# A graph layer on one core: 16-bit column addresses, more columns copied per octet, and the octet's nodes copied on the chip

## The chip, the core and the metric

The kernel runs on one core of a Trainium2 chip. A core has TensorE (PE, matrix products; PEld is its weight load), VectorE (DVE), ScalarE (ACT), GpSimd (POOL) and SyncE (SP, which only issues transfers). Each has its own queue of instructions; they meet through semaphores. Data lie in SBUF (128 partitions), products in PSUM, inputs in HBM. The metric is the device time of the one core in microseconds. Three runs of the kernel before took 3439.3 to 3445.99 us, median 3443.22.

## The reference

One message-passing layer of a graph network, with a residual and a layer norm: 12500 nodes with 64 features, 400000 edges with 16 features, edges sorted by their target `dst`.

```
m_in     = concat([x[src], x[dst], edge_attr], -1)
h        = silu(m_in @ W1 + b1)
messages = silu(h @ W2 + b2)
agg      = segment_sum(messages, dst, 12500)
z        = silu(concat([x, agg], -1) @ W3 + b3)
out      = layernorm(x + z)
```

All is float32. `x[src]` is a gather with random indices; `x[dst]` and the sum are local, since `dst` is sorted.

## The kernel before

**Tiles and octets.** The 400000 edges are 3125 tiles of 128 edges. Eight tiles are an octet (`OT`); there are 391 octets (`NO`). Three octets are a chunk (`CT`), for which target indices and edge features are loaded at once (`load`, tiles `dr` and `oh`). The loop over octets is written out, and inside `tc.manual_schedule` the order on TensorE, ScalarE, VectorE and SyncE is the order of the code. Iteration `o` works on several octets in different stages: the first layer of octet `o`, the second of `o - 2`, the sums over targets of `o - 4`, and preparations for `o + 1` to `o + 3`.

**An octet's stages.** `compare_dst` (L447, VectorE) builds a one-hot matrix that says which of the 48 nodes of the octet's window an edge has as target. `window_load` (L415, SP) brings x of these 48 nodes, transposed and twice, into the tile `xr`; `window_product` (L420, TensorE) multiplies it by the part of W1 for targets; `window_copy` (L425, VectorE) puts the product into one of three weight tiles `xw`. `first_layer` adds up, in PSUM, the transposed gathered rows (L476) and the product of `xw` with the one-hot matrix and the edge features (L480); ScalarE applies silu (L483, `h`). `second_layer` does the same with W2 (L492, L494, silu at L498, `m`). `compare_nodes` (L453, VectorE) builds the one-hot matrix for the sum; `add_up` (L507, TensorE) makes the sums of an octet in `pg`; `add_window` (L512, VectorE) adds them to the resident sums `agg` at a column read from a register.

**Where x[src] comes from.** From octet `RAW` = 12 on, a table `pa = x @ W1[:64]` lies in HBM. Three sources share the edges:

- POOL gathers most tiles with one indirect DMA per tile (`gather`, L396), three octets ahead.
- In the octets of the list `pairs`, the first two tiles are not gathered. Their 256 columns of x are copied out of `xs`, x transposed, which is resident in SBUF, into a tile `cx` (`columns`: ScalarE L303, VectorE L301), one copy of four bytes in 64 partitions per edge. The address of each copy is a register. The registers are filled by loads (L294) from a row of addresses in SBUF, 16 or 8 at a time. TensorE multiplies `cx` by W1 (L479).
- In the octets of `rpairs`, two more tiles come as single rows of `pa`, one SP transfer each (`rows`, L347), 16 per octet.

ScalarE copies `ACOLS` = 32 + 28 columns per octet, before the two silus, and VectorE `VCOLS` = 32 + 32, behind `compare_dst` and behind `compare_nodes`. These are 124 per octet, so a pair of tiles takes 2.06 octets. `index` loads the 256 source indices of a pair as 32-bit integers (SP, L374), `address` (L382, VectorE, two operations of 128) makes addresses of them in place: 4 x index plus the base of `xs`, and, for the second tile, plus a partition offset. For that second tile `xs` holds x a second time in partitions 64 to 127, loaded in octets 5 to 8 (`resident(1, c)`).

**Nodes.** When the sums of 512 nodes are complete, they go through `node_load`, `node_product` (L539 to L542), `node_silu` (L548, tile `z`), `node_stats` (L555 to L559) and, in batches, the norm (`divide`, L572) and `store`. Which octet does which of these is worked out beforehand and kept in the dictionary `todo`; it is run at the end of an iteration.

**Order on VectorE in an iteration:** `add_window`, `compare_dst`, `columns` part 0, `window_copy`, `compare_nodes`, `columns` part 1, `address`, node work. On ScalarE: columns part 0, h, columns part 1, m, node work. On SP: `index`, `rload`, `load` of a chunk two octets ahead, `window_load` three octets ahead, `rows`.

Of the kernel before, what the change touches and what calls it, by code (L numbers as in the profile page):

```python
# [9 lines left out]
F32 = mybir.dt.float32  # L10
BF16 = mybir.dt.bfloat16
I32 = mybir.dt.int32
U8 = mybir.dt.uint8
AF = mybir.ActivationFunctionType
OP = mybir.AluOpType
AX = mybir.AxisListType
# [2 lines left out]
ENG = mybir.EngineType  # L19

P = 128
# [9 lines left out]
LAST = 6  # L31
RAW = 12
TABLES = 7
ACOLS = (32, 28)
VCOLS = (32, 32)
ROWS = 16
LOADS = (16, 8)
XBASE = (0, 64 << 18)
XADDR = 36864
LAG = CT * P // 32  # L40

U = 125
# [58 lines left out]
def windows(ctx, tc, ident, badi, pa, x, xt, src_c, src_row, dst_c, dst_row, attr_t, dst_2, attr_2, base, w1, b1, w2, b2, w3, b3, out, edges):  # L101
# [5 lines left out]
    NO = base.shape[1]  # L107
    assert 2 * (S + A) == P and N + S <= NP
    E = 2 * S
    const = ctx.enter_context(tc.tile_pool(name="fconst", bufs=1))  # L110

    fast = ctx.enter_context(tc.tile_pool(name="fast", bufs=1))
    scp = ctx.enter_context(tc.tile_pool(name="scp", bufs=3))
    srcs = {}

    def sources(k, part=None):
# [24 lines left out]
        nc.scalar.dma_start(w1d[h, h], w1[0:D, :])  # L141
        nc.scalar.dma_start(b1s[h, :], b1.rearrange("(k o) -> k o", o=1))
    XC = 2048
    xs = fast.tile([P, NP], F32, name="xs")

    def resident(s, c):
        w = min(XC, NP - c)
        nc.scalar.dma_start(xs[s * D:(s + 1) * D, c:c + w], xt[:, c:c + w])

    resident(0, 0)  # L150
    for s in range(2):
        h = slice(s * D, (s + 1) * D)
        nc.scalar.dma_start(w2d[h, h], w2)
    resident(0, XC)
    w3x = const.tile([D, D], F32, name="w3x")
    b3r = const.tile([1, G, D], F32, name="b3r")

# [93 lines left out]
    with tc.tile_pool(name="gat", bufs=AHEAD + 2) as gat, tc.tile_pool(name="drp", bufs=2) as drp, \  # L251
# [4 lines left out]
            tc.tile_pool(name="ps1", bufs=2, space=PSUM) as ps1, \  # L256
            tc.tile_pool(name="ps2", bufs=2, space=PSUM) as ps2, \
            tc.tile_pool(name="psa", bufs=1, space=PSUM) as psa, \
            tc.tile_pool(name="cx", bufs=4) as cx, tc.tile_pool(name="cxi", bufs=3) as cxi, \
            tc.tile_pool(name="rx", bufs=2) as rx, tc.tile_pool(name="rxi", bufs=2) as rxi, \  # L260
            tc.tile_pool(name="nx", bufs=2) as nx, tc.tile_pool(name="nv", bufs=1) as nv:
        got, loaded, made = {}, {}, {}
# [2 lines left out]
        RATE = sum(ACOLS) + sum(VCOLS)  # L265
        pairs = []
        while True:
            o = RAW + -(-2 * P * (len(pairs) + 1) // RATE) + 1
            if o >= len(octs) - 1:
                break  # L270
            pairs.append(o)
        cols, indices = {}, {}
        xb = xs.bitcast(U8)

        def columns(o, eng, part):
            if o < RAW:
                return
            lo = (o - RAW) * RATE
            if eng == ENG.Activation:
                lo, n = lo + sum(ACOLS[:part]), ACOLS[part]  # L280
            else:
                lo, n = lo + sum(ACOLS) + sum(VCOLS[:part]), VCOLS[part]
            hi, todo = lo + n, n
            while lo < hi:
# [9 lines left out]
                _, regs = nc.values_load_multi_w_load_instructions(  # L294
                    indices[j][0:1, e0:e0 + n], engines=(eng,), min_val=XBASE[s] + XADDR,
                    max_val=XBASE[s] + XADDR + 4 * (N - 1), skip_runtime_bounds_check_because="src names a node")
                for e, r in zip(range(e0 % P, e0 % P + n), regs):
                    to, frm = t[h, 4 * e:4 * e + 4], xb[h, ds(r - (XBASE[s] + XADDR), 4)]
                    if eng == ENG.DVE:

                        nc.vector.tensor_reduce(to, frm[:, :, None], AX.X, OP.max)  # L301
                    else:
                        nc.scalar.copy(to, frm)  # L303
                lo += n


        def begun(o):

            first, behind = -(-(o - RAW) * RATE // (2 * P)), -(-(o + 1 - RAW) * RATE // (2 * P))
            return range(max(0, first), max(0, min(behind, len(pairs))))  # L310

        def index(o):
            for j in begun(o):
                t = cxi.tile([1, 2 * P], I32, name="cxi")
                e = octs[pairs[j]][1] * P
                nc.sync.dma_start(t, src_row[:, e:e + 2 * P])
                indices[j] = t

        def address(o):
            for j in begun(o):  # L320
                t = indices[j]
                for s in range(2):
                    h = slice(s * P, (s + 1) * P)
                    nc.vector.tensor_scalar(t[:, h], t[:, h], 4.0, float(XBASE[s] + XADDR), op0=OP.mult, op1=OP.add)

        rpairs = []
        while True:
# [48 lines left out]

        def address(o):
            for j in begun(o):
                t = indices[j]
                for s in range(2):  # L380
                    h = slice(s * P, (s + 1) * P)
                    nc.vector.tensor_scalar(t[:, h], t[:, h], 4.0, float(XBASE[s] + XADDR), op0=OP.mult, op1=OP.add)  # L382

        winrow, winreg = {}, {}
        sums = psa.tile([P, 4, S], F32, name="pg")
# [15 lines left out]
        def bases(eng, o):  # L401

            n = min(4, NO - o)
            _, regs = nc.values_load_multi_w_load_instructions(
                bi[0:1, o:o + n], engines=(eng,), min_val=0, max_val=N - 1,
                skip_runtime_bounds_check_because="dst names a node")
            for i in range(n):
                winreg[eng, o + i] = regs[i]

        def window_load(o):  # L410
            if o % 4 == 0:
                bases(ENG.SP, o)
            xr = win.tile([D, 2, S], F32, name="xr")
            frm = xt[:, ds(winreg.pop((ENG.SP, o)), S)]
            nc.sync.dma_start(xr, frm[:, None, :].to_broadcast([D, 2, S]))  # L415
            winrow[o] = xr

        def window_product(o):
# [5 lines left out]
        def window_copy(o):  # L424
            nc.vector.tensor_tensor(xw[o % 3][:E, :], winrow.pop(o)[:E, :], mask[:E, :], op=OP.mult)  # L425
# [159 lines left out]
        todo = {}  # L585

        def later(o, f, *a):
            todo.setdefault(min(o, NO), []).append((f, a))
# [4 lines left out]
        for q in range(early):  # L593
            o = lead[due[q]] + LAST - 1 if q < rest else NO
            later(o - 1, node_load, q)
            later(o, node_product, q)
            later(o, node_silu, q)
            later(o + 2, node_stats, q)
        for q0, q1 in batches:
            o = lead[due[q1 - 1]] + LAST - 1  # L600
# [22 lines left out]
        with tc.manual_schedule(engines={ENG.PE, ENG.Activation, ENG.DVE, ENG.SP}):  # L623
            compare_dst(0)
            compare_nodes(0)
            for o in range(NO + THIRD):
# [5 lines left out]
                    nc.scalar.activation(agg[:, k:k + n], zero.to_broadcast([P, n]), AF.Copy)  # L632
                if o < 2:
                    for c in parts[2:5] if o == 0 else parts[5:]:
                        resident(0, c)
# [7 lines left out]
                if o == RAW:  # L643
                    nc.vector.memset(mv, 1.0)
                    nc.vector.memset(eps, 1e-5)
                if 5 <= o < 5 + (len(parts) + 1) // 2:
                    for c in parts[(o - 5) * 2:(o - 4) * 2]:
                        resident(1, c)
                index(o + 3)
                rload(o + 3)  # L650
                if o % (SCT // OT) == 6 and (o // (SCT // OT) + 1) * SCT < TILES:
                    sources(o // (SCT // OT) + 1)
                if o + AHEAD < NO:
                    gather(o + AHEAD)
                if o + 2 < NO and octs[o + 2][3] and o + 2:
                    load(octs[o + 2][0])
                if o + 3 < NO:
                    window_load(o + 3)
                if o + 1 < NO:
                    window_product(o + 1)  # L660
                if o % 4 == 0 and 4 <= o < NO + 4:
                    bases(ENG.DVE, o - 4)
                if o >= LAST:
                    add_window(o - LAST)
                if o + 1 < NO:
# [1 line left out]
                columns(o, ENG.DVE, 0)  # L667
                if o < NO:
                    first_layer(o)
                if o == 0:  # L670
                    nc.vector.tensor_copy(b2r, b2p[:, None, :].to_broadcast([3, OT, D]))
                if o + 1 < NO:
                    window_copy(o + 1)
                    compare_nodes(o + 1)
                columns(o, ENG.DVE, 1)
                if o == 1:
                    relative(CT, SCT)
                if 10 <= o < 9 + len(cuts):
# [38 lines left out]

        for o in range(NO + THIRD - LAST, NO):
            add_window(o)
        for f, a in todo.get(NO, []):  # L720
            f(*a)
        for q in range(early, NG):
            node_load(q)
            node_product(q)
            node_silu(q)
            node_stats(q)
# [262 lines left out]
```

## Time and profile before

| what | us |
|---|---|
| median of three runs | 3443.22 |
| the profiled execution | 3453.06 |
| its span | 3450.7 |
| ScalarE busy | 2717.7 |
| POOL busy | 2569.0 |
| TensorE matmul busy | 2554.8 |
| VectorE busy | 2517.4 |

The granted TensorE clock was 0.68 of full speed over the span. A row of a group gives the source line, the engine, the operation, output and inputs, the shape and the count; then the busy time in us and the mean duration of one in ns; then how long the engine idled just before, and what ended most of that. "Issue" means that the engine waited for nothing that the profile shows. Short operations overlap in the records, so that the mean of one is longer than the time from start to start. Register loads are not counted as busy.

### The profile page before, as it was taken

To read this page: it belongs to the slowest core of one execution; us is meant where nothing else is said; L and a number is where in the kernel's file an instruction comes from. 1 tells how busy PE (TensorE), PEld (TensorE's weight loads), DVE (VectorE), ACT (ScalarE), POOL (GpSimd) and SP (SyncE) were. 2 spreads that over 40 slices of the span, in tenths; PEclk is the share of its full clock that TensorE was granted. 3 is DMA by queue.
4 is the path that set the end of the run, shared out by engine and by line. 5 is a ranking of instruction groups with operands and counts; after the bars stand their busy time and mean duration, and the time that the engine had idled before them with its cause. 6 is when DMAs were issued, how large, how long until landed. Compare 5 with 4: busy or idle time off the path is not lost. (4 is left out here: it accounts for less than half of the span.)

```text
span 3450.7 us, 104586 instructions
## 1 busy us (share of the span) xinstructions
PE 2554.8 (74%) x13750; PEld 1649.2 (48%) x13750; DVE 2517.4 (73%) x26396; ACT 2717.7 (79%) x23405; POOL 2569.0 (74%) x2724
## 2 busy tenths in 40 slices
PE   6877777777777677776777777777777677677777
PEld 4444544444445445444444445444445454444454
DVE  2477777777777777777777777777777777777775
ACT  2388788788887887888878888887788777878886
POOL 7777777777777777777777777777777777777773
PEclk9666667666667666776666666666666666766767
DMA  7423323323332332333332332333323323333322
GB/s 159 95 53 68 63 59 65 65 61 60 77 61 61 68 62 60 65 65 65 64 69 59 62 68 61 62 75 61 62 60 69 60 61 66 69 62 62 67 61 52
DMA packets 203931, 229.79 MB, mean 67 GB/s; under 512 B 133612, under 2 KB 141988, under 8 KB 202324
## 3 DMA queue, kind: packets, MB, share of 16 engines
q1 hardware_dynamic: 101528, 122.61, 16.1%
q0 software_dynamic: 86880, 89.14, 14.1%
q10 hardware_dynamic: 14812, 11.26, 1.4%
q14 instruction: 595, 4.87, 0.5%
q8 instruction: 116, 1.90, 0.2%
HBM read 216.36 MB, written 6.40 MB: 65 GB/s over the span
## 5 line engine op out<-in xcount | busy, mean ns | idle before, releaser
L396 POOL DMA_INDIRECT ga<-pa,sc x2619 | 2475.4, 945 | 802.2 <-issue 711.9
L303 ACT COPY cx<-xs 64x4 uint8 x22560 | 2216.5, 188 | 166.8 <-issue 122.0
L301 DVE TENSOR_REDUCE cx<-xs 64x4 uint8 x24032 | 1782.6, 150 | 544.7 <-issue 477.8
L507 PEld LDWEIGHTS pg<-eh,m 128*64 128x64 f32 x6250 | 301.0, 182 | 1046.8 <-issue 331.1
L507 PE MATMUL pg<-eh,m 128*64 128x48 f32 x6250 | 351.3, 271 | 580.9 <-DVE agg L512 523.0
L480 PE MATMUL p<-oh,xw 128*128 128x512 f32 (+1 forms) x758 | 601.0, 887 | 132.3 <-DVE xw L425 130.0
L494 PE MATMUL p<-w2d,h 128*128 128x128 f32 x3126 | 674.8, 383 | 0.0
L494 PEld LDWEIGHTS p<-w2d,h 128*128 128x128 f32 x3126 | 573.8, 275 | 133.1 <-issue 133.1
L498 ACT ACTIVATE m<-p 128x512 f32<-128x512 f32 x391 | 232.2, 594 | 255.5 <-PE p L494 249.0
L447 DVE TENSOR_TENSOR oh<-dr,wrow 96x512 f32<-96x512 int32 x391 | 264.4, 676 | 209.1 <-DMA dr<-in_dst 121.6
L483 ACT ACTIVATE h<-p,b1s 128x512 f32<-128x512 f32 x391 | 267.3, 684 | 139.2 <-PE p L480 86.1
L476 PE MATMUL p<-ident,ga 128*128 128x128 f32 x1310 | 336.9, 389 | 41.4 <-DMA ga<-pa,sc 41.4
L420 PE MATMUL mm<-w1bb,xr 64*96 64x128 f32 x782 | 252.9, 418 | 62.0 <-DMA xr<-in_xt 36.7
L476 PEld LDWEIGHTS p<-ident,ga 128*128 128x128 f32 x1310 | 199.6, 190 | 133.3 <-issue 110.3
L480 PEld LDWEIGHTS p<-oh,xw 128*128 128x128 f32 x758 | 176.7, 287 | 169.3 <-DVE xw L425 168.8
L453 DVE TENSOR_TENSOR eh<-wrow,dc 128x384 f32<-128x384 f32 x391 | 211.7, 541 | 0.0
L420 PEld LDWEIGHTS mm<-w1bb,xr 64*96 64x96 f32 x782 | 134.2, 224 | 140.2 <-issue 61.4
L492 PE MATMUL p<-b2r,one 3*128 3x512 bf16 x391 | 196.4, 502 | 0.0
L512 DVE TENSOR_TENSOR agg<-agg,pg 128x48 f32 x391 | 78.1, 200 | 74.2 <-PE pg L507 40.0
L479 PE MATMUL p<-cx,w1d 128*128 128x128 f32 x364 | 105.2, 387 | 22.7 <-ACT cx L303 22.7
L425 DVE TENSOR_TENSOR xw<-mm,mask 96x128 f32<-96x128 f32 x391 | 109.4, 280 | 13.4 <-PE mm L420 7.6
L396 POOL DMA_INDIRECT ga<-in_x,sc x96 | 91.5, 953 | 30.2 <-issue 27.7
(83 smaller groups left out, 767.6 us busy)
## 6 DMA issues: line engine op xcount, KB each, us to landing
rx<-pa SPq DMA_DIRECT2D x5888, 0.2 KB
dr<-in_dst SPq DMA_DIRECT2D x260, 288.0 KB
ga<-pa,sc POOLq DMA_INDIRECT x2619
oh<-in_attr SPq DMA_DIRECT2D x130, 192.0 KB
xr<-in_xt SPq DMA_DIRECT2D x391, 24.0 KB
xs<-in_xt ACTq DMA_DIRECT2D x12, 512.0 KB
pa<-v ACTq DMA_DIRECT2D x12, 256.0 KB
xa<-in_x SPq DMA_DIRECT2D x24, 128.0 KB
```

Of the source, the lines that this page charges most:

```text
L301: nc.vector.tensor_reduce(to, frm[:, :, None], AX.X, OP.max)
L303: nc.scalar.copy(to, frm)
L396: nc.gpsimd.indirect_dma_start(out=ga[:, i, :], out_offset=None, in_=x if o < RAW else pa[:, :], in_offset=bass.IndirectOffsetOnAxis(ap=sc ...
L420: nc.tensor.matmul(pw[:E, :], winrow[o].rearrange("k s w -> k (s w)"), w1bb.rearrange("k s m -> k (s m)"), start=True, stop=True)
L447: nc.vector.tensor_tensor(oh[:E, :], dr[:, e:e + w], wn[:E, o:o + 1].to_broadcast([E, w]), op=OP.is_equal)
L453: nc.vector.tensor_tensor(eh[:, :n], row[:, None, :].to_broadcast([P, n, S]), rel[:, t0:t0 + n, None].to_broadcast([P, n, S]), op=OP.is_equal)
L476: nc.tensor.matmul(p1[:, i, :], g2.rearrange("p s d -> p (s d)"), ident, is_transpose=True, start=(i == c), stop=False, skip_group_check=True)
L480: nc.tensor.matmul(p1[:, :k], xw[o % 3], oh, start=False, stop=True, skip_group_check=True)
L483: nc.scalar.activation(h[:, :k], p1[:, :k], AF.Silu, bias=b1s)
L494: nc.tensor.matmul(p2[:, 2 * i:2 * i + 2, :].rearrange("p s d -> p (s d)"), h[:, i, :], w2d, start=False, stop=(i == k - 1), skip_group_ch ...
L498: nc.scalar.activation(m[:, :n2], p2[:, :n2], AF.Silu)
L507: nc.tensor.matmul(pg[s * D:(s + 1) * D, :], m[:, i, :], eh[:, i, :], start=(i < 2), stop=(i >= n - 2), skip_group_check=True)
```

## The change

- Addresses become 16-bit. `address` writes 4 x index + 8864 into a new tile `cxa` of type uint16, one operation of 256 instead of two of 128 in place. For that `xs` moves to the front of SBUF (a pool `front`, made first), where all its addresses are below 65536, and the scratch of the gathers is halved (`dynamic_dma_scratch_size` 8192).
- Both tiles of a pair are read from partitions 0 to 63 of `xs`; the second copy of x is no longer loaded.
- `ACOLS` is (40, 32) and `VCOLS` (24, 16, 24, 24): 160 columns per octet, 72 on ScalarE and 88 on VectorE. Register loads take 16 at a time, or the 8 that remain. A pair is due one octet later (`+ 2`).
- VectorE's columns come in four parts: behind `compare_dst`, behind the window load, and two behind `compare_nodes`.
- From `RAW` on, `window_load` is a copy by VectorE from `xs` to `xr`, at a column from a register, placed behind `window_copy`. SP no longer issues that transfer nor loads the base nodes for it. VectorE loads base nodes four octets ahead, and `add_window` uses the same registers.
- A chunk is loaded three octets ahead instead of two.
- `node_silu` moves to the iteration after its product, behind `first_layer`.
- Pools: `scp` 2 instead of 3, `cx` 5 instead of 4, `cxi` 2 instead of 3, `cxa` 3.

```diff
-ACOLS = (32, 28)
-VCOLS = (32, 32)
+ACOLS = (40, 32)
+VCOLS = (24, 16, 24, 24)
 ROWS = 16
-LOADS = (16, 8)
-XBASE = (0, 64 << 18)
-XADDR = 36864
+LOADS = (16, 16)
+XADDR = 8864
...
+    front = ctx.enter_context(tc.tile_pool(name="front", bufs=1))
+    xs = front.tile([P, NP], F32, name="xs")
...
-            o = RAW + -(-2 * P * (len(pairs) + 1) // RATE) + 1
+            o = RAW + -(-2 * P * (len(pairs) + 1) // RATE) + 2
...
                 _, regs = nc.values_load_multi_w_load_instructions(
-                    indices[j][0:1, e0:e0 + n], engines=(eng,), min_val=XBASE[s] + XADDR,
-                    max_val=XBASE[s] + XADDR + 4 * (N - 1), skip_runtime_bounds_check_because="src names a node")
+                    addresses[j][0:1, e0:e0 + n], engines=(eng,), min_val=XADDR,
+                    max_val=XADDR + 4 * (N - 1), skip_runtime_bounds_check_because="src names a node")
                 for e, r in zip(range(e0 % P, e0 % P + n), regs):
-                    to, frm = t[h, 4 * e:4 * e + 4], xb[h, ds(r - (XBASE[s] + XADDR), 4)]
+                    to, frm = t[h, 4 * e:4 * e + 4], xb[:D, ds(r - XADDR, 4)]
...
             for j in begun(o):
-                t = indices[j]
-                for s in range(2):
-                    h = slice(s * P, (s + 1) * P)
-                    nc.vector.tensor_scalar(t[:, h], t[:, h], 4.0, float(XBASE[s] + XADDR), op0=OP.mult, op1=OP.add)
+                addresses[j] = cxa.tile([1, 2 * P], U16, name="cxa")
+                nc.vector.tensor_scalar(addresses[j], indices.pop(j), 4.0, float(XADDR), op0=OP.mult, op1=OP.add)
...
         def window_load(o):
-            if o % 4 == 0:
-                bases(ENG.SP, o)
             xr = win.tile([D, 2, S], F32, name="xr")
-            frm = xt[:, ds(winreg.pop((ENG.SP, o)), S)]
-            nc.sync.dma_start(xr, frm[:, None, :].to_broadcast([D, 2, S]))
+            if o < RAW:
+                if o % 4 == 0:
+                    bases(ENG.SP, o)
+                frm = xt[:, ds(winreg.pop((ENG.SP, o)), S)]
+                nc.sync.dma_start(xr, frm[:, None, :].to_broadcast([D, 2, S]))
+            else:
+                frm = xs[:D, ds(winreg[ENG.DVE, o], S)]
+                nc.vector.tensor_copy(xr, frm[:, None, :].to_broadcast([D, 2, S]))
...
-            later(o, node_silu, q)
+            behind.setdefault(o + 1, []).append(q)
...
-                if 5 <= o < 5 + (len(parts) + 1) // 2:
-                    for c in parts[(o - 5) * 2:(o - 4) * 2]:
-                        resident(1, c)
...
-                if o + 2 < NO and octs[o + 2][3] and o + 2:
-                    load(octs[o + 2][0])
-                if o + 3 < NO:
+                if o + 3 < NO and octs[o + 3][3]:
+                    load(octs[o + 3][0])
+                if o + 3 < RAW:
                     window_load(o + 3)
...
-                if o % 4 == 0 and 4 <= o < NO + 4:
+                if o % 4 == 0 and 4 <= o < RAW + 4:
                     bases(ENG.DVE, o - 4)
+                if o % 4 == 0 and RAW <= o + 4 < NO:
+                    bases(ENG.DVE, o + 4)
...
                 if o < NO:
                     first_layer(o)
+                for q in behind.get(o, []) if o < NO else []:
+                    node_silu(q)
...
                     window_copy(o + 1)
+                    if RAW <= o + 3 < NO:
+                        window_load(o + 3)
+                    columns(o, ENG.DVE, 1)
                     compare_nodes(o + 1)
-                columns(o, ENG.DVE, 1)
+                    columns(o, ENG.DVE, 2)
+                columns(o, ENG.DVE, 3)
...
-    nc = bacc.Bacc("TRN2", target_bir_lowering=False, num_devices=1)
+    nc = bacc.Bacc("TRN2", target_bir_lowering=False, num_devices=1, dynamic_dma_scratch_size=8192)
```

More of the change, by code (lines that the diff above doesn't have):

```diff
@@ L13 @@
 U8 = mybir.dt.uint8
+U16 = mybir.dt.uint16
 AF = mybir.ActivationFunctionType
@@ L109, in windows @@
     E = 2 * S
+    front = ctx.enter_context(tc.tile_pool(name="front", bufs=1))
+    xs = front.tile([P, NP], F32, name="xs")
     const = ctx.enter_context(tc.tile_pool(name="fconst", bufs=1))
     fast = ctx.enter_context(tc.tile_pool(name="fast", bufs=1))
-    scp = ctx.enter_context(tc.tile_pool(name="scp", bufs=3))
+    scp = ctx.enter_context(tc.tile_pool(name="scp", bufs=2))
     srcs = {}
@@ L143, in windows, with resident @@
     XC = 2048
-    xs = fast.tile([P, NP], F32, name="xs")
-    def resident(s, c):
+    def resident(c):
         w = min(XC, NP - c)
-        nc.scalar.dma_start(xs[s * D:(s + 1) * D, c:c + w], xt[:, c:c + w])
-    resident(0, 0)
+        nc.scalar.dma_start(xs[:D, c:c + w], xt[:, c:c + w])
+    resident(0)
     for s in range(2):
@@ L153, in windows @@
         nc.scalar.dma_start(w2d[h, h], w2)
-    resident(0, XC)
+    resident(XC)
     w3x = const.tile([D, D], F32, name="w3x")
@@ L258, in windows @@
             tc.tile_pool(name="psa", bufs=1, space=PSUM) as psa, \
-            tc.tile_pool(name="cx", bufs=4) as cx, tc.tile_pool(name="cxi", bufs=3) as cxi, \
+            tc.tile_pool(name="cx", bufs=5) as cx, tc.tile_pool(name="cxi", bufs=2) as cxi, tc.tile_pool(name="cxa", bufs=3) as cxa, \
             tc.tile_pool(name="rx", bufs=2) as rx, tc.tile_pool(name="rxi", bufs=2) as rxi, \
@@ L271, in windows @@
             pairs.append(o)
-        cols, indices = {}, {}
+        cols, indices, addresses = {}, {}, {}
         xb = xs.bitcast(U8)
@@ L304, in columns @@
                 lo += n
[L307 to L320, printed above, removed]
-                t = indices[j]
-                for s in range(2):
-                    h = slice(s * P, (s + 1) * P)
-                    nc.vector.tensor_scalar(t[:, h], t[:, h], 4.0, float(XBASE[s] + XADDR), op0=OP.mult, op1=OP.add)
         rpairs = []
@@ L378, in address @@
             for j in begun(o):
[L379 to L382, printed above, removed]
+                addresses[j] = cxa.tile([1, 2 * P], U16, name="cxa")
+                nc.vector.tensor_scalar(addresses[j], indices.pop(j), 4.0, float(XADDR), op0=OP.mult, op1=OP.add)
         winrow, winreg = {}, {}
@@ L584, in windows @@
         lead = {c: o for o, (c, t, n, first, last) in enumerate(octs) if first}
-        todo = {}
+        todo, behind = {}, {}
         def later(o, f, *a):
@@ L634, in windows @@
                     for c in parts[2:5] if o == 0 else parts[5:]:
-                        resident(0, c)
+                        resident(c)
                 if o == 3:
@@ L719, in windows @@
             add_window(o)
+        for q in behind.get(NO, []):
+            node_silu(q)
         for f, a in todo.get(NO, []):
             f(*a)
+            if f is node_product:
+                node_silu(*a)
         for q in range(early, NG):
```

## The prediction

> **What bounds the kernel now.** I read the page's head and busy shares first, then the costly groups, then the gathers by stretch of time, then the waits of each engine, and last the records of the two column-copying engines.
>
> ```profile
> span 3450.7 us, 104586 instructions
> PE 2554.8 (74%) x13750; PEld 1649.2 (48%) x13750; DVE 2517.4 (73%) x26396; ACT 2717.7 (79%) x23405; POOL 2569.0 (74%) x2724
> ...
> L396 POOL DMA_INDIRECT ga<-pa,sc x2619 | 2475.4, 945 | 802.2 <-issue 711.9
> L303 ACT COPY cx<-xs 64x4 uint8 x22560 | 2216.5, 188 | 166.8 <-issue 122.0
> L301 DVE TENSOR_REDUCE cx<-xs 64x4 uint8 x24032 | 1782.6, 150 | 544.7 <-issue 477.8
> ```
>
> No engine looks full. But POOL's idle time is "issue": it waits for nobody. The gathers (L396) by stretches of time, columns start:end, length, POOL busy and count, clock, DMA share, GB/s:
>
> ```profile
> 600.00:1200.00 600.00, 453.58 (x481) 0.67 0.31 64
> 1200.00:1800.00 600.00, 453.57 (x481) 0.68 0.31 64
> ```
>
> 481 in 600 us is one per 1.248 us, the same in each stretch: POOL starts a gather as soon as it can. 2619 gathers over the 379 octets from RAW = 12 on are 6.91 per octet, so 8.63 us per octet. 379 x 8.63 = 3271 us; the other 180 us of the span are the first twelve octets (96 gathers, about 120 us), the start and the tail. So span = 180 + 379 x P, with P the octet of whatever is slowest. The profiled execution took 3453.06 us around its 3450.7 us span and stands 10 us above the median of 3443.22, so I take 10 off each span.
>
> What is second? The waits of VectorE and ScalarE (us in total, times, longest):
>
> ```profile
> DVE cx L301 <- issue: 477.8, 1458, 0.9
> DVE oh L447 <- DMA dr<-in_dst: 121.6, 71, 5.6
> ACT m L498 <- PE p L494: 249.0, 188, 3.4
> ACT z L548 <- PE mm L542: 123.2, 24, 7.2
> ```
>
> The first is the price of loading addresses into registers, which is not counted as busy. An octet of VectorE without a wait for another engine shows it (start, length, what, idle before):
>
> ```profile
> 3406.68 0.54 DVE L453 TENSOR_TENSOR eh<-wrow,dc 128x384 f32<-128x384 f32 x1
> 3407.46 1.78 DVE L301 TENSOR_REDUCE cx<-xs 64x4 uint8 x24 [0.23 <-issue]
> 3409.54 0.62 DVE L301 TENSOR_REDUCE cx<-xs 64x4 uint8 x8 [0.30 <-issue]
> 3410.24 0.11 DVE L392 MEMSET ga<- 128x64 f32 x1
> 3410.38 0.20 DVE L512 TENSOR_TENSOR agg<-agg,pg 128x48 f32 x1
> 3410.51 0.68 DVE L447 TENSOR_TENSOR oh<-dr,wrow 96x512 f32<-96x512 int32 x1
> 3411.61 1.78 DVE L301 TENSOR_REDUCE cx<-xs 64x4 uint8 x24 [0.43 <-issue]
> 3413.69 0.62 DVE L301 TENSOR_REDUCE cx<-xs 64x4 uint8 x8 [0.30 <-issue]
> 3414.34 0.29 DVE L425 TENSOR_TENSOR xw<-mm,mask 96x128 f32<-96x128 f32 x1
> 3414.55 0.54 DVE L453 TENSOR_TENSOR eh<-wrow,dc 128x384 f32<-128x384 f32 x1
> ```
>
> From L453 to L453 is 7.87 us, 7.7 without the rare memset. Eight copies in 0.62 us, the last lasting 0.15, start 0.064 us apart. 64 of them are 4.1 us, the four large operations by their starts 1.4 us; the rest, 2.2 us, is exposed register loading. Three rows of register loads on VectorE (min/median/max ns): a load of eight beside the run, the loads of base nodes, and the flag:
>
> ```profile
> L294 DVEq TENSOR_LOAD <-cxi x1: 600/600/600, 1709.6 to 1709.6; - x1
> L404 DVEq TENSOR_LOAD <-bi x98: 340/344/761, 50.5 to 3424.8; - x98
> L95 DVEq TENSOR_LOAD <-badi x1: 309/309/309, 3442.9 to 3442.9; - x1
> ```
>
> One register 309, four 344, eight 597 (median), sixteen 1097 (longest by its own window), but three, the last base nodes, 761. Four adjacent 32-bit words come almost as cheaply as one, each further four cost 252, and a short row is taken singly. So the price goes by blocks of 16 bytes more than by registers.
>
> **The change, part by part.**
>
> *Gathers.* 160 columns per octet instead of 124 make 234 pairs of tiles instead of 182: 104 gathers fewer, 2515 from RAW on, 6.636 per octet, 8.29 us at 1.249. POOL alone would end at 180 + 379 x 8.29 = 3322 us of span. This is the gain if the others keep up.
>
> *ScalarE.* 72 instead of 60 copies; over the run 71.1 instead of 59.5 per octet, 11.6 x 0.095 us (32 copies in 3.13 us less the last) = 1.1 us more. Its busy time is 2717.7 / 391 = 6.95 us, so 8.05 to 8.1. That is under 8.29, with 0.2 left where today 1.9 are idle. Its loads ran behind queued copies and stay there. `node_silu` behind the next first layer takes out the 123 us of z waiting for TensorE (24 times); queued behind that wait were 32 copies and m. The PE waits of m and h, 249 and 86 us, are what is late next.
>
> *Loads of 16-bit addresses.* No row shows one. Sixteen are 32 bytes. Low end: two blocks, as eight words today, 597. High end: sixteen registers, as today, 1097. Between, by the rows: 309 for one, 15 x 12 for more registers (four less one, 35 / 3), 203 for a second block, 0.69 us; for eight, 0.39. I take just under this, being nearer the row of eight words than that of sixteen.
>
> *VectorE's octet.* 86.9 copies x 0.064 = 5.56. L447, L453, L425, L512 by their starts 1.4. The copy of the window (64x96): between L512 (200 ns) and L425 (277 ns), 0.15 beyond overlap, and 0.07 for its address in registers. Address scaling 0.62 x 0.28 (L363, 256 words) = 0.17. Node work 75 us / 391 = 0.19. In the records an operation behind copies into the upper 64 partitions starts 0.195 after the last copy's start, behind copies into the lower 0.064: three groups of copies instead of two, half of them in the upper part, and about as much on entering, 0.3. Exposed loading: four loads of sixteen, three of eight. An eight behind sixteen copies is covered (0.39 against eight queued copies, 0.51). A sixteen behind L447 or L453 nearly; behind L425 and the window copy 0.1; the one behind columns 2 lies bare for 0.4 to 0.5. Together 0.5 with cheap loads, 0.8 with 0.69. Sum 8.3 to 8.6; with loads as today the same gaps are 2.7 and the octet 10.5. I take 8.45.
>
> *Moves.* The window load leaves SP: 0.62 (DMA), 0.06, 0.08, 0.05 and a quarter of a base load (0.56), 0.95 us of an SP octet of about 8.1 (sixteen rows by 0.32, a load of 1.4, the window, a share of dr). Its waits for TensorE's buffers go too. dr and oh are issued one octet earlier, past the window and row DMAs of an octet, which covers most of the 121.6 us that L447 waited; their buffers are two chunks old by then. The window copy stands in front of columns 1 and L453; TensorE needs it two octets later, so nobody waits. Seven loads of the second copy of x fall out of octets 5 to 8, where POOL's 96 gathers cover them: 0. Smaller gather scratch and pools: POOL's waits for its DMAs are 54.9 us in steps of 0.3, its ordinary pace, so 0; if the ring filled, each gather would show a longer step.
>
> The window copy and the gathers may block each other. L382, a one-source operation in SBUF, takes 203/207/470 ns, while L425, which reads PSUM, takes 269/277/290: something stretches the first by up to 0.26. POOL's pace is 1.248 in all stretches. The Trainium skill (SBUF — State Buffer, "Who interferes with whom") says that a one-source fp32 copy in SBUF can take the port pair that GpSimd shares, and that the second to issue blocks fully. By that rule the trace agrees on VectorE's side; POOL would lose time as well.
>
> **Sum.** VectorE, not POOL, sets the octet: 180 + 379 x 8.45 = 3382 us of span, 3372 against the median; I say 3370.
>
> **Rivals.**
>
> *POOL keeps the pace* (chance 0.20): loads at the low end and no new waits, 8.29, 3312. For it: POOL lost nearly nothing to others at VectorE's 7.7 to 8.1. Against: VectorE has no slack at all then.
>
> *POOL is blocked by the window copy* (0.05): 0.2 us per octet, 8.49, 3388. It takes one block of the length of L382 each octet; the trace shows no longer POOL step today with rarer such operations. The rule named above is this one.
>
> *VectorE gets slower than today* (0.20, the other side): the load of sixteen. At 0.72 us with the same covers VectorE reaches 8.63 and the gain is gone; at 0.8 to 0.9 it is 8.75 to 8.95, 3486 to 3562. For it: my middle price stands at the edge, and L512 and L447 still wait at times. Against: dr waits shrink.
>
> *ScalarE sets the octet* (0.06): if the 335 us of PE waits (0.88 per octet) stay whole, 8.1 + 0.88 = 8.98, 3573; more than 0.53 left decides. Against: those waits come from ScalarE being early.
>
> *16-bit loads are no cheaper* (0.07): 10.5, 4150. Taken singly as the row of three was, it would be much worse still. The Trainium skill (Runtime: NRT & Kernel Launch, "Instruction fetch mechanics") gives about 200 ns per register even in bulk. The row of sixteen, 69 each, disagrees; the row of three, 254 each, agrees.
>
> **Numbers.** Forecast case (8.3 to 8.55, 3316 to 3410) 0.37; with the first two rivals faster is 0.62. Within 0.2%, about 7 us and what a measurement of this kernel can tell from no change, 0.05: VectorE at 8.61 to 8.65. The last three rivals make slower 0.33. The range reaches from POOL's bound, less 10 us, to the middle of the slower rival: 3300 to 3540.
>
> **What will show it.** L396 x2515 with the same 1.25 us step: then POOL paces; with waits for TensorE or VectorE in between: the forecast. The load rows of L294: 600 to 700 ns and none at 1097. VectorE's busy share near 90%, ScalarE's 93 to 96%, fewer microseconds of dr and z waits. A window copy of 0.2 us with a tail to 0.45. The prediction is wrong if a load of sixteen takes over 0.75 us, if copies between partition halves start more than 0.064 us apart, or if ScalarE's waits for TensorE stay.

## The result and the profile after

The changed kernel takes 9219.82 us (median of 4, 9218.33 to 9238.71); the kernel before took 3442.43 us beside it (median of 4). The ratio is 2.6795, interval 2.6748 to 2.6841. The forecast of 3370, range 3300 to 3540, is far off and on the wrong side.

The head of the page after, and the three costliest groups that answer to those shown of before:

```profile
span 9218.5 us, 116445 instructions
PE 3029.1 (33%) x13802; PEld 1918.7 (21%) x13802; DVE 3120.7 (34%) x35525; ACT 3288.2 (36%) x27837; POOL 2467.2 (27%) x2620
...
L302 DVE TENSOR_REDUCE cx<-xs 64x4 uint8 x32912 | 2335.0, 140 | 5932.7 <-issue 5925.2
L376 POOL DMA_INDIRECT ga<-pa,sc x2515 | 2373.6, 944 | 6640.5 <-PE p L460 5709.1
L304 ACT COPY cx<-xs 64x4 uint8 x26992 | 2763.7, 188 | 3878.7 <-issue 3378.6
```

The work did change as the diff says: 2515 gathers in place of 2619, 8880 more copies on VectorE, 4432 more on ScalarE. One copy costs no more than it did (140 ns on VectorE, before 150, and 188 on ScalarE as before). But every engine now stands idle for about two thirds of the span, and in front of VectorE's copies lie 5925.2 us of "issue", where before it was 477.8. POOL, which waited for nobody, waits 5709.1 us for TensorE. The waits of all engines (us in total, times, longest) show the chain of blame:

```profile
DVE cx L302 <- issue: 5925.2, 2675, 3.7
PE pg L491 <- DVE agg L496: 5718.8, 373, 18.4
POOL ga L376 <- PE p L460: 5709.1, 352, 26.0
...
ACT cx L304 <- issue: 3378.6, 1796, 3.2
ACT m L482 <- PE p L478: 1940.7, 386, 7.4
```

POOL waits for TensorE to free gathered tiles, TensorE waits for VectorE to add up `agg`, and VectorE waits for nobody: its 2675 waits of at most 3.7 us are "issue". What is being done in them is in the records of line 295, the register loads (ns, min/median/max):

```profile
L295 DVEq TENSOR_LOAD <-cxa x2618: 1820/3582/3847, 130.9 to 9170.8; - x187
L295 ACTq TENSOR_LOAD <-cxa x1968: 1704/3368/3602, 133.5 to 9185.1; - x197
```

A load of sixteen 16-bit addresses takes 3582 ns on VectorE, where a load of sixteen 32-bit ones took 1097; one of eight takes 1820 in place of 597. That is 224 and 228 ns for each register, nearly the same price in both. The greater part of an octet of VectorE in the timeline (start, length, what, idle before):

```profile
4006.45 1.10 DVE L302 TENSOR_REDUCE cx<-xs 64x4 uint8 x16 [3.33 <-issue]
4007.48 0.54 DVE L437 TENSOR_TENSOR eh<-wrow,dc 128x384 f32<-128x384 f32 x1
4010.65 1.10 DVE L302 TENSOR_REDUCE cx<-xs 64x4 uint8 x16 [2.63 <-issue]
4013.03 0.59 DVE L302 TENSOR_REDUCE cx<-xs 64x4 uint8 x8 [1.28 <-issue]
4016.94 1.10 DVE L302 TENSOR_REDUCE cx<-xs 64x4 uint8 x16 [3.31 <-issue]
4019.33 0.60 DVE L302 TENSOR_REDUCE cx<-xs 64x4 uint8 x8 [1.28 <-issue]
```

Sixteen copies last 1.10 us, and 3.3 us of empty engine stand in front of them. An octet has 86.9 copies on VectorE, 86.9 x 0.224 = 19.5 us of loading; by the prediction's own relation the octet is (9218.5 - 180) / 379 = 23.85 us. The loads last four fifths of it, and 5925.2 / 379 = 15.6 us of the octet are empty engine in front of copies.

### The profile page after: what moved, and what is told of

It reads as the page before. It is cut to its first block, busy times and chain, and to the rows that moved or that the text cites. A ratio compares the mean times of both kernels' runs of the same rounds, so it can differ in the third digit from the quotient of the medians.

```text
span 9218.5 us, 116445 instructions
## 1 busy us (share of the span) xinstructions
PE 3029.1 (33%) x13802; PEld 1918.7 (21%) x13802; DVE 3120.7 (34%) x35525; ACT 3288.2 (36%) x27837; POOL 2467.2 (27%) x2620
## 5 line engine op out<-in xcount | busy, mean ns | idle before, releaser
L302 DVE TENSOR_REDUCE cx<-xs 64x4 uint8 x32912 | 2335.0, 140 | 5932.7 <-issue 5925.2
L376 POOL DMA_INDIRECT ga<-pa,sc x2515 | 2373.6, 944 | 6640.5 <-PE p L460 5709.1
L304 ACT COPY cx<-xs 64x4 uint8 x26992 | 2763.7, 188 | 3878.7 <-issue 3378.6
L491 PE MATMUL pg<-eh,m 128*64 128x48 f32 x6250 | 422.3, 307 | 5734.0 <-DVE agg L496 5718.8
L491 PEld LDWEIGHTS pg<-eh,m 128*64 128x64 f32 x6250 | 370.2, 219 | 6276.2 <-issue 4478.7
L482 ACT ACTIVATE m<-p 128x512 f32<-128x512 f32 x391 | 233.3, 597 | 1943.3 <-PE p L478 1940.7
L464 PE MATMUL p<-oh,xw 128*128 128x512 f32 (+1 forms) x758 | 719.2, 1049 | 404.1 <-DVE xw L409 403.9
L478 PE MATMUL p<-w2d,h 128*128 128x128 f32 x3126 | 798.9, 436 | 0.0
L478 PEld LDWEIGHTS p<-w2d,h 128*128 128x128 f32 x3126 | 685.0, 323 | 167.9 <-issue 167.9
L437 DVE TENSOR_TENSOR eh<-wrow,dc 128x384 f32<-128x384 f32 x391 | 214.3, 548 | 2.5
L463 PE MATMUL p<-cx,w1d 128*128 128x128 f32 x468 | 145.1, 413 | 0.1
L463 PEld LDWEIGHTS p<-cx,w1d 128*128 128x128 f32 x468 | 126.8, 331 | 0.3 <-ACT cx L304 0.3
```

The lines of the kernel that those rows point to most:

```text
L376: nc.gpsimd.indirect_dma_start(out=ga[:, i, :], out_offset=None, in_=x if o < RAW else pa[:, :], in_offset=bass.IndirectOffsetOnAxis(ap=sc ...
L463: nc.tensor.matmul(p1[:, 0, :], w1d, cols.pop(o), start=False, stop=False, skip_group_check=True)
L464: nc.tensor.matmul(p1[:, :k], xw[o % 3], oh, start=False, stop=True, skip_group_check=True)
L478: nc.tensor.matmul(p2[:, 2 * i:2 * i + 2, :].rearrange("p s d -> p (s d)"), h[:, i, :], w2d, start=False, stop=(i == k - 1), skip_group_ch ...
L482: nc.scalar.activation(m[:, :n2], p2[:, :n2], AF.Silu)
L491: nc.tensor.matmul(pg[s * D:(s + 1) * D, :], m[:, i, :], eh[:, i, :], start=(i < 2), stop=(i >= n - 2), skip_group_check=True)
```

## The experiments

The theory after this result (A): a row of 16-bit values is loaded into registers one value at a time, at about 0.224 us each, whatever else the change does. Rivals: the copies or their new source cost it (B); element size matters, but a row of 32-bit words is fast wherever it lies (C). Behind that stands a second question: what is the rest of the change worth, the moves and the copied columns?

**The type of the address row.** The changed kernel with one word different:

```diff
-                addresses[j] = cxa.tile([1, 2 * P], U16, name="cxa")
+                addresses[j] = cxa.tile([1, 2 * P], I32, name="cxa")
```

> The changed kernel with its addresses kept as 32-bit words; nothing else is undone. Theory A (the 16-bit values are the loss: a load takes aligned 32-bit words four at a time and 16-bit values one by one): loads of sixteen and eight on VectorE fall from 3.58 and 1.82 us to 1.10 and 0.60. VectorE then has 86.9 copies x 0.064 = 5.6, other operations 2.0, exposed loading 2.7 per octet, 10.2 to 10.5 us, and the time is 180 + 379 x 10.3 = 4080 us, 3980 to 4200. So the type is worth some 5100 of the 5780 us lost, and the rest of the change still loses 600. Rival B (the copies out of the lower half of xs, the window copy or the smaller gather scratch cost much as well): loads as in A, but 5000 us or more.

4140.01 us (4129.53 to 4150.49), ratio 1.2017 [1.1979, 1.2055] to before, with the same 2515 gathers and 32912 copies. The loads:

```profile
L295 DVEq TENSOR_LOAD <-cxa x2618: 591/1094/1151, 130.5 to 4080.3; - x187
L295 ACTq TENSOR_LOAD <-cxa x1968: 536/1017/1231, 133.0 to 4091.7; - x197
```

and of the waits, where before and after are to be compared:

```profile
PE pg L491 <- DVE agg L496: 1293.0, 343, 8.7
POOL ga L376 <- PE p L460: 853.1, 265, 12.4
...
DVE cx L302 <- issue: 737.0, 1285, 1.2
```

The type alone costs 9219.82 - 4140.01 = 5080 of the 5777 us lost, and B falls: the copies and their source are the same in both. What is left of the loss, 700 us, is VectorE again: from one L437 to the next it is 10.56 us on average between 600 and 3600 us, against 8.63 of POOL before. 160 columns are too many even with words.

Then the same 32-bit words moved one word along in a longer tile, so that no load starts where it did:

```diff
-                addresses[j] = cxa.tile([1, 2 * P], I32, name="cxa")
+                addresses[j] = cxa.tile([1, 2 * P + 4], I32, name="cxa")[:, 1:1 + 2 * P]
```

> As the run with 32-bit addresses, but the row of addresses begins one word further on, so that no load starts at a multiple of 16 bytes. Theory A (four words at a time only in rows that start and end on 16 bytes, else one by one): a load of sixteen costs about what it cost with 16-bit values, 16 x 0.224 = 3.6 us, and the time is again about 9200 us. Rival C (only the element's size counts): 1.10 us, and the time of the run with 32-bit addresses.

9283.81 us (one execution, span 9282.0). The loads of 32-bit words:

```profile
L295 DVEq TENSOR_LOAD <-cxa x2618: 1837/3599/3854, 142.7 to 9234.2; - x187
L295 ACTq TENSOR_LOAD <-cxa x1968: 1734/3423/3644, 144.1 to 9248.5; - x197
```

So C falls: 32-bit words that start 4 bytes off cost as much as 16-bit values. Cheap are, in these traces, rows of words that start at a multiple of four words of their tile and have four, eight or sixteen of them (344, 597 and 1097 ns before); the row of three base nodes (761 ns before) fits as an odd row, at 254 each. Which length and start exactly decide, no run shows.

The type by itself, with the columns and loads of before (60 and 64) behind the moves of the change:

```diff
-ACOLS = (40, 32)
-VCOLS = (24, 16, 24, 24)
+ACOLS = (32, 28)
+VCOLS = (32, 0, 32, 0)
-LOADS = (16, 16)
+LOADS = (16, 8)
```

> The 16-bit addresses with the column numbers of before (60 and 64 columns, loads of 16 and 8), otherwise the run of the moves alone: the type is the only difference to that run. Theory A (each 16-bit value costs 0.224 us to load on VectorE): 63 columns x 0.224 = 14.2 us of loading per octet, of which what the copies and the large operations cover is little; with 3.6 us of copies behind the loads' ends, the octet is 17.6 us and the time 180 + 379 x 17.7 = 6880 us, 6700 to 7050. Rival (the loads are slow only in numbers, since 160 columns jam the queues): under 5000 us.

6896.44 us (one execution, span 6894.6), inside the expectation. The price goes with the number of registers, not with the number of columns added.

**The moves, without type and columns.** The same three constants as just shown, and I32; all else of the change stays, the single copy of x and the buffers included:

> 32-bit addresses and the column numbers of before (32 + 28 on ScalarE, 32 behind compare_dst and 32 behind compare_nodes on VectorE, loads of 16 and then 8): what is left of the change is the window copy on VectorE, the earlier loads of a chunk, the later node_silu, one resident copy of x and the pools. Theory (the moves help a little, since SyncE loses 0.95 us of its 8.1 us octet, and VectorE with the window copy stays at 7.8 to 8.0 us, under POOL's 8.63): VectorE's 121 us of waits for dr and ScalarE's 123 us of waits for z are mostly gone, POOL paces as before, 3410 to 3440 us. Rival (the moves cost: the window copy stretches VectorE or delays the gathers): POOL's step grows above 1.25 us or VectorE sets the octet, 3450 us or more.

3439.58 us (10 runs), ratio 0.9984 [0.9974, 0.9993]. POOL still starts 480 and 481 gathers in 600 us, and the moves show in the waits rather than the time: of the 121.6 us for dr and the 123.2 us for z 1.5 and 9.6 are left. Instead ScalarE's h waits 359.9 us for TensorE, before 86.1. The first waits now read

```profile
POOL ga L376 <- issue: 747.5, 2452, 0.3
PEld p L460 <- issue: 541.6, 433, 5.6
PE p L460 <- DMA ga<-pa,sc: 490.5, 301, 5.5
```

Before, the third of these was

```profile
PE p L476 <- DMA ga<-pa,sc: 41.4, 23, 4.6
```

TensorE now waits for gathers: the computing engines have caught up with POOL, which alone sets the pace.

**Columns on top of the moves.** 72 on ScalarE and 64 on VectorE, 136 in all, I32:

```diff
-ACOLS = (32, 28)
+ACOLS = (40, 32)
-LOADS = (16, 8)
+LOADS = (16, 16)
```

> As the run with the moves alone, with 40 + 32 columns on ScalarE and 32 + 32 on VectorE, 136 per octet, loads of up to 16. POOL: 6.81 gathers per octet, 8.51 us. ScalarE 67 to 72 copies, 8.0 to 8.1 us. VectorE's copies as before, 7.8 us. Theory (POOL paces, the moves have made room): 180 + 379 x 8.51 = 3405, less some tail and 10 us, 3370 to 3400 us. Rival (ScalarE's octet of 8.1 with its waits for TensorE is too tight): 3440 us or more, with ScalarE waiting for p L494 in most octets.

3391.94 us, ratio 0.9843 [0.9826, 0.9859]; 2585 gathers, ScalarE busy 3172.0 us or 93%. And four more on VectorE, `VCOLS = (32, 0, 36, 0)`, 140 in all:

> The run with 136 columns, and 36 instead of 32 columns behind compare_nodes on VectorE: 140 per octet. POOL 6.78 gathers, 8.47 us. VectorE's octet rises by four copies and a load of four to 8.0 to 8.2, ScalarE's is 8.06. Theory (POOL still paces): 379 x 0.04 = 15 us less than with 136, 3372 to 3385 us. Rival (three engines within 5% of the octet get into each other's way): 3392 us or more, POOL waiting for TensorE.

3381.36 us (3380.52 to 3385.03), ratio 0.9823 [0.9807, 0.984]: the fastest kernel of the study, faster than both. POOL is at its own pace in it, by stretches of time (start:end, length, busy and count, clock, DMA share, GB/s):

```profile
600.00:1200.00 600.00, 453.66 (x480) 0.71 0.30 62
1200.00:1800.00 600.00, 453.96 (x480) 0.71 0.30 63
```

**Columns without the moves.** The kernel before with `ACOLS = (40, 32)` alone:

> The kernel before with 40 + 32 columns on ScalarE instead of 32 + 28, nothing else. POOL alone would need 8.50 us per octet, as in the run of the changed kernel with 136 columns and 32-bit addresses. Theory (in the kernel before, SyncE with 8.1 us per octet and VectorE waiting for its dr hold the octet at 8.7 whatever POOL does; the moves made the room): 3430 to 3455 us, POOL waiting for TensorE. Rival (the moves are worth nothing, the gain is the columns'): 3385 to 3400 us.

3499.93 us, ratio 1.017 [1.0153, 1.0187]: slower than before, against both expectations. The same with `LOADS = (16, 16)`, as the changed kernel has them:

> The kernel before with 72 columns on ScalarE (136 in all) and with ScalarE's and VectorE's address loads in runs of sixteen throughout, as in the run of 136 columns behind the moves (3391.94). With loads of eight behind the first sixteen the same kernel took 3499.93. If the shorter loads were what held it back, this one comes to 3400 to 3440. If the places of the steps are (VectorE waits 202.0 us for dr in that run, and TensorE for the sums behind it), it stays at 3480 to 3510. I expect the latter.

3486.07 us, ratio 1.0121 [1.0098, 1.0144]. The loads of eight were not the reason. From about 1200 us on POOL falls under its pace there, by stretches of time:

```profile
600.00:1200.00 600.00, 451.62 (x479) 0.66 0.31 64
1200.00:1800.00 600.00, 435.67 (x461) 0.65 0.32 63
```

So something in the change makes room for 12 more columns, some 94 us at 136 columns (3486.07 to 3391.94). The next runs look for it. First each named move put back alone, in the kernel of 136 columns. The window by SyncE's DMA again (its body and the loads of base nodes go back with it, not shown):

```diff
-                if o + 3 < RAW:
+                if o + 3 < NO:
                     window_load(o + 3)
...
-                    if RAW <= o + 3 < NO:
-                        window_load(o + 3)
```

> The run with 136 columns and 32-bit addresses, but the window comes by SyncE's transfer again, with its base loads; the other moves stay. Theory (it is SyncE's 0.95 us that made the room): SyncE is at 8.1 of 8.5 us, dr and window come late, 3410 to 3445 us, with VectorE and TensorE waiting for DMA. Rival (the earlier chunk loads and the later node_silu made it): 3385 to 3400 us, and SyncE keeps up.

3408.15 us, ratio 0.9902 [0.9885, 0.9918], between the two expectations: 16 us of the 94. TensorE now waits for the window, with its weight loads 538.2 us and with its products 416.6 us:

```profile
PEld mm L400 <- DMA xr<-in_xt: 538.2, 146, 9.1
...
PE mm L400 <- DMA xr<-in_xt: 416.6, 131, 10.3
```

Then `node_silu` right behind `node_product`, and the chunk loads an octet later, each alone:

```diff
-            behind.setdefault(o + 1, []).append(q)
+            later(o, node_silu, q)
```

> The 136 columns behind the moves (3391.94), with node_silu put back right behind node_product alone. ScalarE then waits for z again: 91.9 us in 25 waits in the run of 136 columns without the moves, here 11.6 in 2. ScalarE is 93% busy, so I expect most of that difference on the path: 3400 to 3460. If ScalarE is not what sets the octet, under 3400.

```diff
-                if o + 3 < NO and octs[o + 3][3]:
-                    load(octs[o + 3][0])
+                if o + 2 < NO and octs[o + 2][3] and o + 2:
+                    load(octs[o + 2][0])
```

> The 136 columns behind the moves (3391.94), with the chunk loads (dr, oh) put back by one octet alone. If the early chunk load is what makes the room, VectorE waits for dr again (202.0 us in 86 waits without the moves, here 1.8 in 2), and the time is 3430 to 3490. If SyncE, which now has no window to load, issues them in time anyway, under 3405.

3387.22 us, 0.9838 [0.9818, 0.9859], and 3389.18 us, 0.9843 [0.9822, 0.9863]: neither is worth anything by itself. For `node_silu` I had expected 3400 to 3460, and that was wrong; for the loads two outcomes were on record, and the one under 3405 came. In both POOL keeps its pace, with TensorE waiting 497.8 and 536.1 us for gathers, so there is slack to lose. All three put back together:

> The 136 columns with all three moves put back: window loaded by SyncE's DMA, chunk loads an octet later, node_silu right behind node_product. What is left of the change is one copy of x, one operation for the addresses, other buffer counts and loads of sixteen. If the three places of steps make all the room, 3480 to 3510, as the kernel before with 136 columns (3499.93). If what is left makes part of it, in between 3400 and 3480.

3404.77 us, 0.9878 [0.9851, 0.9905]. VectorE waits 189.7 us for dr again, as in the kernel before, and yet 81 of the 94 us remain (3486.07 to 3404.77). The moves that I had in view are not what makes the room.

One more step of the change is left in that kernel: a pair of copied tiles is used an octet later. Alone in the kernel before with 136 columns (with the fifth `cx` buffer that it needs), and undone alone in the last kernel:

```diff
-            o = RAW + -(-2 * P * (len(pairs) + 1) // RATE) + 1
+            o = RAW + -(-2 * P * (len(pairs) + 1) // RATE) + 2
```

> The kernel before with 136 columns and loads of sixteen (3486.07), and one thing of the change: a finished pair of copied tiles is used one octet later (the + 2 for the + 1, with a fifth buffer for it). Without it TensorE waits 112.7 + 85.8 us for ScalarE's columns in that run; with it and the rest of the change, but none of the three moved steps, the time was 3404.77. If the octet of room for the pairs is what that rest is worth, 3400 to 3425. If it is the single copy of x, the one address operation or the buffer counts, it stays at 3470 to 3490.

> The reverse: all that is left of the change when the three moves are put back (136 columns, 3404.77), and the pairs used one octet earlier, as before. If the octet of room for the pairs is the cause, 3460 to 3490 and waits of TensorE for ScalarE's columns near 200 us again. If not, 3400 to 3415.

3479.14 us, 1.0106 [1.0076, 1.0135], and 3406.65 us, 0.9898 [0.9875, 0.9922]: it isn't that either.

What remains is the single copy of x, one operation for the addresses in a tile of their own, buffer counts, and the DMA scratch with the place of x. The pages of 3486.07 and 3404.77 name two suspects: VectorE is busy 2437.6 us in the one and 2385.8 in the other, of which its copies are 1706.8 and 1669.2, and SyncE's wait for ScalarE's address loads before it may bring a new row (L374), 81.7 us over the run, is gone in the second. Whether either lay on the path, the pages do not show. Four runs went to these, in the kernel before with 136 columns. The fourth buffer of indices (`cxi` 3 to 4, `scp` 3 to 2):

> The kernel before with 136 columns (3486.07) and a fourth buffer for the row of indices (a third chunk buffer of sources given up for the room). SyncE's load of a new row (L374) waits 28.9 us in the middle 1800 us until ScalarE has loaded the last addresses out of the old one, 15 waits of up to 3.6, and dr and the later loads stand behind it on SyncE. In the changed kernel the addresses have a tile of their own and that wait is gone. If it makes the room: 3400 to 3430. If not, 3475 to 3490.

The single copy of x (both halves read `xb[:D, ...]`, one `tensor_scalar` over the row):

> The kernel before with 136 columns (3486.07), columns of both halves copied out of one copy of x, and one operation for the addresses of a pair of tiles in place of two. It takes 0.62 x 0.2 = 0.13 us off VectorE's octet of 8.77: if VectorE sets the octet, 3430 to 3440; if reading the second copy costs more than the rows show, under 3430; if the cause is elsewhere, 3475 to 3490.

Both:

> Both together: the single copy of x with one address operation, and the fourth buffer of indices. If each makes a part, below both single runs, at best 3400 to 3415 as in the changed kernel without the three moves (3404.77).

The scratch alone (`dynamic_dma_scratch_size=8192`):

> The kernel before with 136 columns (3486.07) and only the smaller DMA scratch of the change (8192). The prediction put it at nothing: 3475 to 3490. If the scratch matters to the gathers, under 3450.

They don't answer it. They ran on another chip than the rest, on which the kernel before itself took 5264.19 us (7 runs), and beside it the four took, in this order, 5454.44, 5393.91, 5447.78 and 6629.21 us, ratios 1.0362 [1.0345, 1.038], 1.0248 [1.0231, 1.0265], 1.0356 [1.0327, 1.0385] and 1.2586 [1.2564, 1.2608]. Copies and gathers have their usual mean length there (188 or 189, 141 to 152 and 944 ns), but ScalarE stands still between operations that wait for nobody, here in the timeline of the single copy of x:

```profile
2000.71 0.29 ACT L303 COPY cx<-xs 64x4 uint8 x2 [1.12 <-issue]
2001.44 0.19 ACT L303 COPY cx<-xs 64x4 uint8 x1 [0.44 <-issue]
2002.15 0.60 ACT L496 ACTIVATE m<-p 128x512 f32<-128x512 f32 x1 [0.52 <-issue]
```

VectorE's copies break off at the same moments (starts at 2000.72, 2001.45, 2002.16). What holds both is not in the records. The stops are longest in the scratch run, which has 158821 instructions where the other three have about 107400: 2635.8 us in front of ScalarE's copies against 1495.0 to 1510.7. Whether the number of instructions is the reason, no run tested. A kernel bound by this says nothing of the room in the others, so which of the remaining parts makes the 81 us stays open.

The last of the four, the scratch, changed more than was meant. The records of the copying lines have a row each that no other kernel has:

```profile
L303 ACTq ALU_OP  x27000: 3/35/1472, 229.2 to 6595.4; - x199
...
L301 DVEq ALU_OP  x23944: 3/40/1617, 223.2 to 6583.5; - x200
```

One register operation for each copy. By the code, the register holds the finished address `4 * src + XADDR`, and the copy takes `XADDR` off again and adds the place of x; nothing is left to add when x lies at `XADDR`. With the smaller scratch x must lie elsewhere. In the change `XADDR` moves along (36864 becomes 8864), and its trace has no such row. So this run added work of its own, and the scratch's price by itself is not measured; the gathers lose nothing by it, since POOL keeps 480 or 481 of them in 600 us in the kernels of 124, 136 and 140 columns that have the smaller scratch.

## Why the prediction was wrong, point by point

**The failed step: "Loads of 16-bit addresses".** It bounded a load of sixteen between 597 and 1097 ns and took just under 0.69 us. Measured are 3582 ns, 3.3 times the upper end, and far over the 0.75 us that the prediction itself named as its sign of being wrong. What failed is the rule behind both ends, that the price goes by blocks of 16 bytes and that a 16-bit register costs at worst what a 32-bit one does. The runs showed a price for each register in its place: 224 ns for 16-bit values and for words 4 bytes off, and 68 to 69 ns only for the aligned words of before and of the run with I32.

The trace of before had a row outside both ends: three base nodes in 761 ns, 254 each. The prediction read it rightly, "a short row is taken singly", then used 1097 as the upper end all the same. Priced by that row, sixteen are 4.1 us, the loading of VectorE's octet is 86.9 x 0.254 = 22 us, and the time is above 8500 us (180 + 379 x 22). No row of before could say which of the two a row of 16-bit values would follow, so the dear one belonged in the range.

The rival "16-bit loads are no cheaper" has the right mechanism in its second sentence, "Taken singly as the row of three was, it would be much worse still", with no price and a share of 0.07. The Trainium skill (Runtime: NRT & Kernel Launch, "Instruction fetch mechanics") gives some 200 ns for each register even in bulk. The changed kernel's 224 ns come near that, the 68 to 69 ns of the aligned words do not.

**The rest of VectorE's octet** was right in total. The sum gave 10.5 us "with loads as today" at 160 columns; the run with I32 measured 10.56, 4140 us against the rival's 4150. Its terms were not measured one by one.

**ScalarE**, 8.05 to 8.1 predicted, is 3172.0 / 391 = 8.11 with 72 columns. The rival in which its waits for TensorE stay whole did not come true once ScalarE was full: m's and h's were 249.0 and 86.1 us before and are 26.1 and 51.6 in the 136-column kernel behind the moves. In the changed kernel itself m's are 1940.7 us, because TensorE there is late behind VectorE.

**The window copy** was right: 0.2 us with a tail to 0.45 was forecast, and this is its row in the changed kernel:

```profile
L399 DVE COPY xr<-xs x379: 187/192/429, 111.9 to 9179.1; 64x96 f32 x190
```

The rival "POOL is blocked by the window copy" is false: with that copy in each octet the 140-column kernel still starts 480 gathers in 600 us, as many as before within one. So whatever stretches the copy to 0.43 us costs POOL nothing that shows: a gather lasts 947 ns on average there, 945 before. The Trainium skill (SBUF — State Buffer, "Who interferes with whom") lets either side block the other; no run here shows POOL losing time to the copy.

**The moves** were judged by their waits, and those went as said: dr and z. But the waits were not on the path. The moves, with all else of the change but type and columns, bring 0.16% [0.07%, 0.26%], two of the three can each be undone at no loss, and the window load is worth 16 us at 136 columns. The prediction didn't name the later use of the copied pairs; it proved worth no more than a few us either way.

**The gathers**: 2515 was right, and span = 180 + 379 x P holds within about 0.5% where POOL sets P. At 140 columns, 2573 / 379 x 1.249 = 8.48, it gives 3394 of span, and 3379.7 was measured.

## What to carry to other kernels

A register load is not priced by bytes: on VectorE sixteen 32-bit words that start at a multiple of four words cost about 70 ns each here, and the other rows of several registers that these runs had (16-bit, three words, one word off) about 225 to 254 ns each. When one row of a trace doesn't fit the rule that you draw from the others, it belongs in the range as an end, above all for an operation that no row shows. And a wait that disappears is not time that is won: ask first whether the waiting engine sets the pace.

## What the runs showed of the hardware

- Register loads of a 16-bit row, and of a 32-bit row 4 bytes off, are priced by the register: 3582 and 3599 ns for sixteen on VectorE, 3368 and 3423 (medians) on ScalarE; aligned words 1094 and 1017.
- A copy whose source lies in partitions 0 to 63 and whose target lies in 64 to 127 costs no more: VectorE's copies are 140 ns on average with one copy of x in the lower half, 150 with two.
- One chip ran the kernel before in 5264 us in place of some 3440. The traces of the four kernels run there show copies and gathers at their usual length; the piece above has common stops of ScalarE and VectorE of 0.4 to 1.2 us. The cause is not in the traces.
